# Cross-attention of layer 0: who copies keys and queries out of PSUM, and in which order three small projections are issued

## The chip, the cores and the metric

The kernel is one program on one core of one Trainium2 chip. The metric is the device time of one execution in microseconds (us). It is compared as a median of runs; the profile comes from one further execution.

## The reference, cut to what matters

A decoder of two layers on 32 batches of 100 tokens of width 256, with a context of 361 rows of width 128 for each batch. In order: self-attention, cross-attention and a mixture of experts in layer 0, then the same three in layer 1, each behind a layer norm and with a residual. The change lies in the cross-attention of layer 0 alone:

```python
Q = (x @ Wq.T).reshape(B, xN, 16, 16)
KV = (z @ Wkv.T).reshape(B, zN, 2, 16, 16)
K, V = KV[:, :, 0], KV[:, :, 1]
attn = softmax(einsum('bqhd,bkhd->bhqk', Q, K) * 0.25)
O = einsum('bhqk,bkhd->bqhd', attn, V).reshape(B, xN, 256) @ Wo.T
x = x + O
```

Sixteen heads of only 16 channels: a head fills 16 of the 128 rows of the systolic array, so the kernel packs four pairs of heads into four row groups of 32.

## The kernel before, in words

Each stage is a method; `l0_xattn` (L478 to L725) is the one that the change touches. Everything is f32.

**The two copies.** A row group of 32 channels holds two heads, "even" (j = 0) and "odd" (j = 1). Queries and keys are kept twice, as `t[:, c, 0, :]` and `t[:, c, 1, :]`. In each copy one head of the pair is kept and the other head's rows are overwritten: with zeros for queries (scale `quarter`, 0.25 or 0), with a row of ones and zeros for keys (scale `own`, bias `one`). The row of ones lets a second multiplication subtract the row maximum for nothing. `queries` (L543, 128x400 for four batches at once) and `keys` (L552, 128x361 for one batch) multiply into one PSUM bank and copy that bank out twice; before the change ScalarE makes both copies (L550, L557). `vals` (L561) is copied out by ScalarE too, in two or four pieces (L570).

**The loop** (L694) runs over M = 0 to 65; batch b = M // 2, group of eight heads c = M % 2. I call one pass a *step*. TensorE's order is exactly the order of the code (`manual_schedule` for PE). In a full step M it issues:

1. `maxima(M-1)` (L588): two transposes of the negated row maxima (L593) into one bank; VectorE adds them to the queries, giving `q2` (L595).
2. `scores(M, 0)` (L576): four matmuls of 100x361 into four banks, and four VectorE reductions (L585), one for each bank.
3. `divided(M-3)` (L636): a VectorE reciprocal (L638) and GpSimd products into `zT` (L642).
4. `turned(M-1, 0)` (L597): twelve matmuls of keys by `q2` into four banks, then four exponentials on ScalarE (L607) and two sums on GpSimd (L611, L612).
5. `values(M-2)` (L614): 24 + 8 small matmuls (L621, L628) into one bank, copied out by ScalarE (L633).
6. `scores(M, 1)` and `turned(M-1, 1)`, as above.
7. The *extras* of the step (L716). Even M: keys for group 0 of the next batch (K), the output projection of a finished tile of 128 rows (O, where one is finished: `out`, L644, whose result VectorE adds to x in L283 and whose norm statistics follow in L219 and L222), and two thirds of the values (V). Odd M: keys for group 1 (K), queries (Q, in two of every eight steps), the last third of the values (V).
8. Where something is pending in `later`, a turn of normalised rows (N: L253, copied out by `evac`, alternately by ScalarE, L172, and VectorE, L173) or the gate of the mixture of experts (G, whose VectorE part begins with L1534 and goes on with L1538 to L1547). The rows themselves are normalised by VectorE ahead of item 2 (L231, two instructions in the steps named in `norms`, L675).

**The banks.** All PSUM tiles of this stage come from one pool of eight banks (`banks("l0x", t=8)`, L481; `bank` sends every tag to "t"). A step takes 20 to 22 of them, so a bank is reused within half a step, and a matmul waits until the readers of the tile that had the bank before are done. In particular the four banks of `turned(M-1, 0)` are those of the extras of the step before and of `maxima`.

**The other queues.** ScalarE, VectorE and GpSimd each run their instructions in one fixed order, which a scheduler chose when the program was built. An instruction that waits holds up all that stand behind it on its engine.

Of the kernel before, what the change touches and what calls it, by code (L numbers as in the profile page):

```python
# [12 lines left out]
AF = mybir.ActivationFunctionType  # L13
ALU = mybir.AluOpType
# [10 lines left out]
L = 361  # L25
# [96 lines left out]
class Kernel:  # L122
# [355 lines left out]
    def l0_xattn(self):  # L478
        nc, tc, a = self.nc, self.tc, self.a
        with ExitStack() as st:  # L480
# [14 lines left out]
            for h in range(H):  # L495
# [16 lines left out]
            own, quarter, one = (  # L512
                cp.tile([P, 2], F32, tag=n, name=n) for n in ("own", "quarter", "one")
            )
# [24 lines left out]
            def load(b):  # L539
                ctx[b] = pool.tile([CD, LP], F32, tag="cT", name="cT", bufs=3)  # L540
                nc.sync.dma_start(ctx[b], a["ctxT"][:, b, :])

            def queries(b0, c):  # L543
                if c == 0:
                    q[b0 // 4] = pool.tile([P, 2, 2, 4 * T], F32, tag="qT", name="qT")
                pm = self.bank_t()[:, : 4 * T]
                self.mm(pm, [(wq[:, k, c * P : (c + 1) * P], self.xn_of(k, b0, 4)) for k in range(NK)])
                t = q[b0 // 4]
                for j in range(2):
                    nc.scalar.activation(t[:, c, j, :], pm, AF.Copy, scale=quarter[:, j : j + 1])  # L550

            def keys(b, c):  # L552
                pm = self.bank_t()[:, :L]
                self.mm(pm, [(wk[:, c * P : (c + 1) * P], ctx[b][:, :L])])
                t = ks[b % 3]
                for j in range(2):
                    nc.scalar.activation(  # L557
                        t[:, c, j, :L], pm, AF.Identity, bias=one[:, j : j + 1], scale=own[:, j : j + 1]
                    )

            def vals(b, c0, n):  # L561
                pm = self.bank_t()[:KC0, : n * D].rearrange("p (c d) -> p c d", c=n)
                for i in range(n):
                    c = c0 + i
                    self.mm(pm[:, i, :], [(ctx[b][:, c * KC0 : (c + 1) * KC0], wv)])
                pv = pm.rearrange("p c (h j d) -> p c h j d", j=2, d=16)
                v = vs[b % 3][:, c0 : c0 + n].rearrange("p c (h j) e -> p c h j e", j=2)
                for j in range(2):
                    for i in range(n):
                        nc.scalar.copy(v[:, i, :, j, 16 * j : 16 * j + 16], pv[:, i, :, j, :])  # L570
# [5 lines left out]
            def scores(M, j):  # L576
                b, c = divmod(M, 2)
                cols = slice((b % 4) * T, (b % 4 + 1) * T)
                ps = [self.bank("r")[:T, :L] for _ in range(4)]
                for r in range(4):  # L580
                    self.mm(ps[r], [(q[b // 4][rows_of(r), c, j, cols], ks[b % 3][rows_of(r), c, j, :L])])
                m = ms[M % 3]
                for r in range(4):
                    o = 32 * r + 16 * (1 - j)
                    got = nc.vector.tensor_reduce(m[:, j, o : o + 1], ps[r], AX.X, ALU.max, negate=True)  # L585
                return got

            def maxima(M):  # L588
                b, c = divmod(M, 2)
                cols = slice((b % 4) * T, (b % 4 + 1) * T)  # L590
                pt = self.bank_t()[:, : 2 * T].rearrange("p (j t) -> p j t", j=2)
                for j in range(2):
                    nc.tensor.transpose(pt[:, j, :], ms[M % 3][:, j, :], self.ident[:T, :T])  # L593
                q2[M] = pool.tile([P, 2, T], F32, tag="q2", name="q2")
                self.after = nc.vector.tensor_tensor(q2[M], pt, q[b // 4][:, c, :, cols], ALU.add)  # L595

            def turned(M, j):  # L597
                b, c = divmod(M, 2)
                ps = [self.bank("r")[:KC0, : NKC * T] for _ in range(4)]
                for i in range(NKC):  # L600
                    for r in range(4):
                        self.mm(ps[r][:, i * T : (i + 1) * T], [(
                            ks[b % 3][rows_of(r), c, j, i * KC0 : (i + 1) * KC0], q2[M][rows_of(r), j, :]
                        )])
                t = e[M, j] = pool.tile([KC0, 4, NKC, T], F32, tag="e", name="e", bufs=5)
                for r in range(4):
                    nc.scalar.activation(t[:, r], ps[r].rearrange("p (c t) -> p c t", c=NKC), AF.Exp)  # L607

                n = L - 2 * KC0
                s = es[M, j] = pool.tile([KC0, 4, T], F32, tag="es", name="es", bufs=4)  # L610
                nc.gpsimd.tensor_tensor(s, t[:, :, 0, :], t[:, :, 1, :], ALU.add)  # L611
                nc.gpsimd.tensor_tensor(s[:n], s[:n], t[:n, :, 2, :], ALU.add)  # L612
# [23 lines left out]
            def divided(M, zs, after):  # L636
                b, c = divmod(M, 2)
                got = nc.vector.reciprocal(zs[:, 1, :], zs[:, 1, :])  # L638
                if after is not None:
                    self.depend(got, [after.ins], "behind the maxima, whose banks are waited for")  # L640
                for z, cols in self.z_parts(b):
                    nc.gpsimd.tensor_tensor(z[:, c, :], zs[:, 0, cols], zs[:, 1, cols], ALU.mult)  # L642

            def out(f):  # L644
                self.out_proj(f, wo)
                self.norm_stats(f, EDGES)
# [14 lines left out]
            def extras(b):  # L661

                k0, k1, v0, v1, o, x = [None] * 6
                if b + 1 < NB:
                    k0, k1 = (lambda: keys(b + 1, 0)), (lambda: keys(b + 1, 1))
                    v0, v1 = (lambda: vals(b + 1, 0, 2)), (lambda: vals(b + 1, 2, 1))
                if b > 1 and tile_of(b - 2) is not None:
                    o = lambda: out(tile_of(b - 2))
                b0, i = b // 4 * 4, b % 4
                if i < 2 and b0 + 4 < NB:  # L670
                    x = lambda: queries(b0 + 4, i)
                return k0, v0, o, k1, v1, x
# [11 lines left out]
            with tc.manual_schedule(engines={mybir.EngineType.PE}):  # L684
                load(0)
                load(1)
                for c in range(2):
                    queries(0, c)
                for c in range(2):
                    keys(0, c)  # L690
                vals(0, 0, 2)
                vals(0, 2, 1)
                last = 2 * NB
                for M in range(last + 2):  # L694
                    b, c = divmod(M, 2)
                    if c == 0:
                        if b + 2 < NB:
                            load(b + 2)
                        ex = extras(b)
                    if 0 < M <= last:  # L700
                        maxima(M - 1)
                    if M in norms:
                        f, *at = norms[M]
                        f(*at)
                    for j in range(2):

                        got = scores(M, j) if M < last else None
                        if j == 0 and M > 2:
                            divided(M - 3, zs, got)
                        if 0 < M <= last:  # L710
                            turned(M - 1, j)
                        if j == 0 and M > 1:
                            zs = values(M - 2)
                    if M == last + 1:
                        divided(M - 2, zs, None)
                    for i in (0, 2, 1):  # L716
                        if ex[3 * c + i]:
                            ex[3 * c + i]()
                    if M not in norms or len(later) > 3:
                        for _ in range(1 + (len(later) > 3)):  # L720
                            if later:
                                later.popleft()()
                out(NF - 1)
                while later:
                    later.popleft()()  # L725
# [1496 lines left out]
```

## Time and profile before

| what | value |
|---|---|
| median of 3 runs | 2894.04 us (2893.76 to 2896.32) |
| the profiled execution | 2872.93 us, of which 2871.0 us are the profile's span |
| granted TensorE clock, mean of the span | 0.986 |
| first and last score matmul of layer 0's cross-attention | 526.0 us and 1002.3 us after the span's start |
| first transposes of the maxima, L593, to the last | 530.7 us to 1006.0 us |
| VectorE, mean of one: L585 (100x361 reduction) / L595 / L638 | 525 / 366 / 778 ns |
| ScalarE, mean of one: L557 (keys) / L550 (queries) / L607 / L570 | 679 / 621 / 426 / 298 ns |

A line of the timeline reads: start and length in us, engine, line of the kernel, operation, what it writes and reads, shape, and how many instructions were merged into the line; in brackets the idle time of the engine ahead of it and what ended it. The profiled execution is 1.9 us longer than its span (2872.93 against 2871.0). The profiled execution was 0.7% shorter than the median of the timed runs.

### The profile page before, as it was taken

Reading aid. Unit: us, or ns where it says so; the run is one execution under the profiler, and the core shown is the slowest. Engines: PE = TensorE matmul, PEld = TensorE weight load, DVE = VectorE, ACT = ScalarE, POOL = GpSimd, SP = SyncE. Lnnn points to the kernel's source line nnn. Section 1 sums busy time; section 2 is a strip of 40 time slices with the busy share of each in tenths; the row PEclk is TensorE's granted clock in tenths of the full one; section 3 lists DMA queues with packets and bytes.
Section 4 is the critical chain, followed back from the end, with each engine's and each line's share of the span. In section 5 each row is a group of like instructions: output and inputs, shape, how many; then the busy total and the mean of one; then the engine's idle time right before and its main releaser. Section 6 shows DMA issues by size and latency. Waiting matters only on the chain. (4 is left out here: it accounts for less than half of the span.)

```text
span 2871.0 us, 66274 instructions
## 1 busy us (share of the span) xinstructions
PE 2768.8 (96%) x25880; PEld 2150.2 (75%) x25880; DVE 1760.6 (61%) x5043; ACT 1391.4 (48%) x4210; POOL 920.4 (32%) x1079
## 2 busy tenths in 40 slices
PE   8999999999999999999999999999999999999992
PEld 7888888777777757888886777777777777776672
DVE  7666766677777742222225877677676676766553
ACT  5555655666667621222223225656565566567220
POOL 3222212465656544222211330021311202123473
PEclk9999999999999989999999999999999999999997
DMA  7444333000000033655652210010000000000496
GB/s 246 134 131 165 133 141 120 23 16 16 13 16 16 5 107 137 204 199 190 203 219 92 80 43 10 9 43 18 27 15 9 12 12 11 13 11 5 122 216 190
DMA packets 133877, 242.02 MB, mean 84 GB/s; under 512 B 40714, under 2 KB 105925, under 8 KB 126768
## 3 DMA queue, kind: packets, MB, share of 16 engines
q1 hardware_dynamic: 103488, 143.53, 16.0%
q0 software_dynamic: 26784, 90.83, 9.8%
q8 instruction: 209, 3.42, 0.5%
q10 hardware_dynamic: 3280, 3.28, 0.3%
q14 instruction: 116, 0.95, 0.1%
HBM read 152.12 MB, written 111.18 MB: 92 GB/s over the span
## 5 line engine op out<-in xcount | busy, mean ns | idle before, releaser
L1818 POOL DMA_INDIRECT x_d<-xr,slot x200 | 195.0, 975 | 657.4 <-ACT eT L846 595.1
L178 PE MATMUL ps_t<-xnT,wA 128*128 128x200 f32 (+1 forms) x1608 | 322.5, 348 | 2.2 <-DMA wA<-in_wq 1.6
L178 PE MATMUL ps_t<-cT,q 128*128 128x361 f32 (+1 forms) x832 | 306.1, 470 | 0.0
L846 ACT COPY eT<-ps_t 124x384 f32<-124x384 f32 x400 | 191.2, 486 | 221.1 <-PE ps_t L845 221.0
L178 PEld LDWEIGHTS ps_t<-xnT,wA 128*128 128x128 f32 x1608 | 273.0, 191 | 30.2 <-issue 14.6
L836 ACT ACTIVATE wBx<-ps_t,m 128x361 f32<-128x361 f32 x400 | 227.5, 570 | 119.5 <-DVE m L833 115.2
L585 DVE TENSOR_REDUCE m<-ps_t 100x1 f32<-100x361 f32 x512 | 239.6, 525 | 47.4 <-PE ps_t L178 47.2
L178 PE MATMUL ps_t<-xT,w 128*128 128x256 f32 (+1 forms) x1276 | 260.2, 364 | 0.7 <-ACT xT L172 0.7
L178 PEld LDWEIGHTS ps_t<-xT,w 128*128 128x128 f32 x1276 | 223.8, 190 | 36.0 <-issue 9.3
L833 DVE TENSOR_REDUCE m<-ps_t 128x1 f32<-128x361 f32 x400 | 210.9, 528 | 59.3 <-PE ps_t L178 57.1
L845 PEld LDWEIGHTS ps_t<-ident,wBx 128*124 128x124 f32 x1200 | 150.2, 139 | 117.6 <-issue 70.5
L607 ACT ACTIVATE e<-ps_t 121x300 f32<-121x300 f32 x512 | 173.9, 426 | 119.0 <-PE ps_t L178 119.0
L384 ACT ACTIVATE e<-s,m 100x100 f32<-100x100 f32 x512 | 185.6, 364 | 66.2 <-DVE m L378 66.2
L388 POOL TENSOR_TENSOR e<-e,rz 100x400 f32<-100x400 f32 x128 | 109.3, 854 | 323.8 <-PE ps_t L178 208.0
L845 PE MATMUL ps_t<-ident,wBx 128*124 128x128 f32 x1200 | 196.8, 275 | 3.6 <-DVE top L1758 2.3
L178 PE MATMUL ps_t<-wA,cT 128*124 128x512 f32 x384 | 195.6, 597 | 0.0
L1465 DVE TENSOR_TENSOR h<-ps_t,g 128x256 f32<-128x256 f32 (+1 forms) x145 | 58.3, 402 | 188.4 <-ACT g L1464 188.4
L838 DVE TENSOR_SCALAR wBx<-wBx,sums 128x361 f32<-128x361 f32 x400 | 165.4, 414 | 9.4
L178 PEld LDWEIGHTS ps_t<-q,k 32*121 32x121 f32 x3072 | 127.6, 181 | 36.1 <-issue 11.3
L1464 ACT ACTIVATE g<-ps_t 128x256 f32<-128x256 f32 (+1 forms) x145 | 52.9, 365 | 190.9 <-PE ps_t L178 190.9
L857 PEld LDWEIGHTS ps_t<-eT,v 124*64 124x64 f32 x3072 | 134.0, 137 | 13.5 <-issue 6.1
L837 DVE RECIPROCAL sums<-sums 128x1 f32<-128x1 f32 x400 | 63.8, 160 | 126.3 <-ACT wBx L836 124.8
(333 smaller groups left out, 5678.1 us busy)
## 6 DMA issues: line engine op xcount, KB each, us to landing
x_d<-fill SPq DMA_DIRECT2D x16, 1284.0 KB
we<-in_wexp SPq DMA_DIRECT2D x32, 384.0 KB
cT<-in_ctxT SPq DMA_DIRECT2D x64, 186.0 KB
xe_d<-zero SPq DMA_DIRECT2D x8, 1028.0 KB
xe<-x_d SPq DMA_DIRECT2D x24, 321.0 KB
sum<-fill SPq DMA_DIRECT2D x10, 640.0 KB
yk<-y_d SPq DMA_DIRECT2D x25, 256.0 KB
xe<-xe_d SPq DMA_DIRECT2D x24, 257.0 KB
```

Source lines behind the costliest of these rows:

```text
L178: self.nc.tensor.matmul(out, lhsT=l, rhs=r, start=(i == 0), stop=(i == n - 1))
L384: nc.scalar.activation(t[:, i, :], s[:, i, :], AF.Exp, bias=m[:, i : i + 1], accum_out=rz[:, i : i + 1])
L388: nc.gpsimd.tensor_tensor(t[:, h, :], t[:, h, :], self.last(rz[:, h], T), ALU.mult)
L585: got = nc.vector.tensor_reduce(m[:, j, o : o + 1], ps[r], AX.X, ALU.max, negate=True)
L607: nc.scalar.activation(t[:, r], ps[r].rearrange("p (c t) -> p c t", c=NKC), AF.Exp)
L833: self.after = nc.vector.tensor_reduce(m, ps, AX.X, ALU.max, negate=True)
L836: nc.scalar.activation(t, ps, AF.Exp, bias=m, accum_out=z)
L838: nc.vector.tensor_scalar(t, t, z, None, ALU.mult)
L845: nc.tensor.transpose(pt[:, c, :], es[n % 5][:, c * KC : (c + 1) * KC], self.ident)
L846: self.after = nc.scalar.copy(eT[:, :, o : o + P], pt)
L857: nc.tensor.matmul(pz[64 * j : 64 * j + 64, i, :], lhsT=v[:, c, h * 64 : (h + 1) * 64], rhs=eT[:, c, o : o + T], start=(c == 0), stop=(c = ...
L1818: got = nc.gpsimd.indirect_dma_start(out=self.x1_d[:, :], out_offset=bass.IndirectOffsetOnAxis(ap=slot[:, j, k : k + 1], axis=0), in_=xr[: ...
```

## The change

```diff
                 t = q[b0 // 4]
-                for j in range(2):
-                    nc.scalar.activation(t[:, c, j, :], pm, AF.Copy, scale=quarter[:, j : j + 1])
+                nc.scalar.activation(t[:, c, 0, :], pm, AF.Copy, scale=quarter[:, 0:1])
+                nc.vector.tensor_scalar_mul(t[:, c, 1, :], pm, quarter[:, 1:2])
...
                 t = ks[b % 3]
-                for j in range(2):
-                    nc.scalar.activation(
-                        t[:, c, j, :L], pm, AF.Identity, bias=one[:, j : j + 1], scale=own[:, j : j + 1]
-                    )
+                nc.scalar.activation(t[:, c, 0, :L], pm, AF.Identity, bias=one[:, 0:1], scale=own[:, 0:1])
+                nc.vector.tensor_scalar(t[:, c, 1, :L], pm, own[:, 1:2], one[:, 1:2], op0=ALU.mult, op1=ALU.add)
...
-                    for i in (0, 2, 1):
+                    for i in ((0, 1, 2), (2, 0, 1))[c]:
                         if ex[3 * c + i]:
                             ex[3 * c + i]()
```

The copies with j = 1 go to VectorE: 64 of keys and 16 of queries. The extras are issued in the order K, V, O in even steps (before: K, O, V) and Q, K, V in odd steps (before: K, Q, V).

The scheduler of the other engines gives VectorE a new order with it. GpSimd's and the DMA queue's orders are the same as before; ScalarE's is the same but for the copies that went, the Q and K that changed places, and a few places near the stage's end. As built, VectorE's queue from the last reduction of a step to the first of the next is (`q2` is L595, "K2" and "Q2" the new copies):

```
step                             before                            after
even, O                          L283 L219 L222 q2                 K2 L283 q2 L219
even, O and G                    L283 L219 L222 L1534 q2           K2 L283 L1534 L219 L1538 x2 L222 L1539 x2 q2
even, no O                       q2                                K2 q2
odd, Q                           q2                                Q2 q2 K2
odd, Q, rows to normalise next   q2 L231 L231                      Q2 q2 K2 L231 L231
odd, N copied by VectorE         L173 q2                           K2 L173 q2
odd, N copied by ScalarE         q2                                K2 q2
```

In the program after, K2 and Q2 carry a wait for ScalarE's semaphore: each starts only when ScalarE's copy of the same bank is done. (Of the odd steps without Q, N or G, some have K2 behind q2.)

## The prediction

> **What bounds the kernel now.** I read the page's busy shares first, then the busy times of one window, then the waits in it, and last the timeline, step by step.
>
> ```profile
> PE 2768.8 (96%) x25880; PEld 2150.2 (75%) x25880; DVE 1760.6 (61%) x5043; ACT 1391.4 (48%) x4210; POOL 920.4 (32%) x1079
> 530.46:1005.60 475.14, 464.75 (x8721) 361.75 (x8720) 359.24 (x871) 322.31 (x929) 285.64 (x361) 1.00 0.05 14
> ```
>
> TensorE (PE) bounds the whole, and this stage too: 464.75 us busy of 475.14 (the row's columns are length, PE, its weight loads, VectorE, ScalarE, GpSimd). VectorE (DVE) is busy 359 us, ScalarE (ACT) 322 us, so the change takes work from the freer engine and gives it to the fuller one. What counts is therefore only where TensorE waits for either. The longest pieces of the chain that ended last all lie behind 1531 us and say nothing of this stage, so I take the waits from 530 to 1010 us:
>
> ```profile
> PEld ps_t L178 <- DVE m L585: 9.9, 56, 0.5
> PEld ps_t L178 <- ACT v L570: 8.0, 14, 1.1
> PEld ps_t L621 <- DVE m L585: 8.0, 14, 1.4
> PE ps_t L621 <- DVE m L585: 5.7, 7, 1.2
> ...
> PEld ps_t L178 <- ACT k L557: 2.5, 6, 0.6
> ...
> PE ps_t L178 <- ACT v L570: 1.9, 10, 0.2
> ...
> PEld ps_t L178 <- ACT qT L550: 1.4, 4, 0.4
> ```
>
> The first number is us in total. On ScalarE's copies TensorE waits 8.0 + 2.5 + 1.9 + 1.4 = 13.8 us: the most that the change can give back, and 0.5% of the time. On VectorE's reductions it waits 23.6 us already. A step without stalls takes 6.5 to 7.5 us by its extras; I compared each step, cut at the first transpose of the maxima, with the shortest of its kind.
>
> **What is removed and added.** ScalarE loses 64 key copies and 16 query copies. A pair of key copies takes 1.22 us and one 0.68, so a queue step of ScalarE is 0.54 us shorter. VectorE gets 80 instructions that the trace does not show. Nearest rows: a VectorE instruction with a pointer scalar from PSUM takes 408 ns at 128x200 (L348) and 478 ns at 128x256 (L2092); extended at 1.04 ns an element that is 0.58 us for 128x361 and 0.62 for 128x400. Bounds: 0.44 (what each of four reductions of the same width in a row adds, 1.85 us in all) and 0.68 (ScalarE's copy). I take 0.58, of which the queue behind it sees 0.49, as reductions of 0.525 follow at 0.44.
>
> The new copy K2 waits for ScalarE's copy of the same bank, and that stands behind four exponentials. Here is the end of odd step 21, where VectorE also copies a turn of rows (N), and the start of step 22:
>
> ```profile
> 681.12 1.85 DVE L585 TENSOR_REDUCE m<-ps_t 100x1 f32<-100x361 f32 x4 [0.34 <-PE ps_t L178]
> ...
> 681.74 1.36 ACT L607 ACTIVATE e<-ps_t 121x300 f32<-121x300 f32 x4 [0.99 <-PE ps_t L178]
> ...
> 682.95 1.22 ACT L557 ACTIVATE k<-ps_t,one,own 128x361 f32<-128x361 f32 x2
> ...
> 683.29 0.34 PE L593 MATMUL ps_t<-ident,m 100*128 100x100 f32 x2
> 683.49 0.69 DVE L173 COPY xnT<-ps_t 128x512 f32<-128x512 f32 x1 [0.52 <-PE ps_t L253]
> ...
> 684.10 0.35 DVE L595 TENSOR_TENSOR q<-ps_t,qT 128x200 f32<-128x200 f32 x1
> ...
> 684.60 1.01 PE L178 MATMUL ps_t<-q,k 32*121 32x100 f32 x24 [0.18 <-ACT v L570]
> ```
>
> Read it as a race into q2 (L595), which TensorE's twelve `turned` matmuls (684.60) need. VectorE is free at 682.97 and idle to 683.49. K2 cannot use that gap: ScalarE's first copy ends at 682.95 + 0.68 = 683.63. So K2 runs 683.68 to 684.26, L173 goes from 683.49 to 684.17, q2 from 684.10 to 684.78.
>
> **A, N by VectorE:** q2 0.68 later, `turned` about 0.65 (it had 0.15 behind q2, 0.05 is enough). Steps 6, 14, 22, 30, 54: 3.3; step 42 (Q in front, more slack) 0.3. Together **+3.6**.
>
> **B, rows to normalise.** In step 20 q2 runs at 669.83, L231 twice from 670.23, the reductions from 670.88; the first ends at 671.40 and TensorE's `values` (L621), which take that bank, start at 671.48. After the change K2 stands between q2 and L231 and moves this by 0.49 less the slack. Steps 4, 12, 20, 28, 36, 44, 52: seven times 0.45; step 24 0.3. **+3.5**.
>
> **C, O with a gate (G).** End of step 26, start of 27:
>
> ```profile
> 722.10 1.03 PE L178 MATMUL ps_t<-wB,cT 128*121 128x256 f32 x4
> 722.30 0.42 DVE L283 TENSOR_TENSOR x_sb<-ps_t,x_sb 128x256 f32<-128x256 f32 x1 [0.51 <-PE ps_t L178]
> ...
> 723.96 0.17 DVE L1534 COPY lg<-ps_t 128x16 f32<-128x16 f32 x1 [0.55 <-PE ps_t L178]
> ...
> 724.18 0.37 DVE L595 TENSOR_TENSOR q<-ps_t,qT 128x200 f32<-128x200 f32 x1
> 724.47 0.23 DVE L1538 MAX8 top<-lg 128x8 f32<-128x8 f32 x2
> 724.66 0.09 DVE L1539 MATCH_VALUE_LOAD ti<-top,lg 128x8 f32 x1
> ...
> 724.76 0.79 PE L178 MATMUL ps_t<-q,k 32*121 32x100 f32 x24
> ```
>
> With V ahead of O, O ends where V ended, 723.13 instead of 722.26. L283 moves there, and its statistics no longer fit ahead of L1534 (it waits for G in any case). The built order then runs L219 (0.4), L1538, L222, L1539 (0.49 from 724.47 to the next reduction, and 0.1) before q2: it starts near 725.03, not 724.18. Steps 27, 43, 47: 0.8 each; 39 and 55, where VectorE was late before behind q2 and gets that part back, 0.4. **+3.2**.
>
> **D, square roots.** In steps 19, 35, 51 the norm's statistics feed a ScalarE square root ahead of the exponentials (two table loads of 1.28 us). It waits for L224, which ended at 661.93 with O first; with O last, and q2, L219, two reductions and L222 ahead of it, near 663.54. The square root ran at 663.02, so the exponentials come 0.55 later: **+1.6**.
>
> **E, O alone** (steps 7, 9, 11, 15, 17, 21, 25, 29, 33, 37, 45, 53). In step 20 L283 goes from 676.24 to 677.11, q2 ends at 677.85 instead of 677.64; `turned` started 0.21 behind q2, so 0 to 0.2 is lost. I take 0.1: **+1.2**.
>
> **What comes back.** F, the start: four query and four key copies (2.05 + 2.30 us) halve, the first scores start 0.4 us earlier, the first exponentials 0.5: -0.9. G, N copied by ScalarE (8, 16, 38, 46): TensorE loses 0.64 to K and the turn; q2 now ends 0.5 later behind K2 and takes back half: -1.2. H, steps 3, 5, 13, 41, 49 lose 0.57 to V's copies. ScalarE is earlier by 0.54, but K2 ends at 618.1 in step 12, so q2 goes from 617.50 to 618.01, the stall only changes its name: -0.5. I, steps 10, 18, 34, 50, 32, 48, 56: ScalarE's stall of 0.3 to 0.5 gone, K2 behind q2 in its place: -0.7. J, steps 40 and 60: one reduction now stands ahead of the rows: -0.9. Together **-4.2**.
>
> Sum: 3.6 + 3.5 + 3.2 + 1.6 + 1.2 - 4.2 = **+8.9 us**. Against the profiled execution that is 2872.93 to 2881.8; against the median 2894.04, which is 0.7% above that execution, 2902.9. Steps 57 to 61, with gate, root and rows at once, I leave at 0 (2 either way). GpSimd's and the DMA queue's order and work do not change; later stages start as much later as this one ends.
>
> The Trainium skill, "PSUM — Partial Sum Buffer", section "PSUM bank collisions raise a hardware error", says that two engines must not access one bank at once, reads included, so that software has to put one behind the other. It speaks against the change's idea, two copies side by side; the trace of before has no bank that both read freely. Could both read at once, K2 would fit VectorE's gap at 682.97 and A and the loss in G would be gone: the sum by that would be about +4. A second rule, "SBUF — State Buffer", section "SBUF: two separate sides", says that VectorE and GpSimd lock each other out of a shared port for some instructions; were K2 one of these, it could cost what L231 does beside GpSimd.
>
> **Rivals.** *Faster: ScalarE's relief decides.* For it: TensorE's waits on ScalarE are 13.8 us, and VectorE is idle a quarter of the stage. If they all go and only B stays, -13.8 + 3.5 = -10: 2884. Against it: the wait of K2 on ScalarE, and q2 behind K2 in VectorE's fixed queue. It decides if q2 starts no later than 0.1 us beyond its place of before in most steps.
> *Nothing:* stalls change their names as in H, and A to E are half hidden: 2891 to 2897.
> *Much slower: K2 is long.* L231 takes 412 ns in the median but up to 1286 ns in this stage beside GpSimd; L348, from PSUM, never over 427. If K2 behaves like L231 and takes 0.5 more in some 25 steps of A, B, C, H: +12, 2915.
>
> **How the numbers follow.** Forecast (sum as worked, 2897 to 2910) 0.57; much slower 0.15; nothing 0.15; faster 0.13. Bounds: K2 at 0.44 or 0.68 moves A and B by -1 to +1.5; E is 0 to 2.4; C and D could be half; G and H could give 4 more. The range, 2889 to 2914, leaves out most of the faster case and the end of the slowest. About 0.2%, 5.8 us, is what a measurement of this kernel can tell from no change. Faster by more: 0.13. Within: the nothing case and a fifth of the forecast, 0.26. Slower: 0.61.
>
> **What would show it.** In the profile after: K2 starts within 0.1 us of the end of ScalarE's key copy and takes 0.5 to 0.6; q2 ends 0.6 later in steps like 22 and 0.8 later in those like 27; TensorE's waits on L570 and L557 shrink while those on L595 and L585 grow. I am wrong if TensorE's busy time over this stage is the same and its steps are shorter, or if K2 starts ahead of ScalarE's end.

## The result and the profile after

The changed kernel takes 2900.77 us, the median of 14 runs (2897.19 to 2906.46). The kernel before, run beside it 14 times, takes 2895.76 us. The ratio is 1.0018, with a 95% interval of 1.0011 to 1.0026: 3.2 to 7.5 us slower, +5.0 in the middle. The prediction had +8.9 us, so the sign is right and the sum is too large. By the prediction's own line of 5.8 us, a change of 5.0 falls under "within" (0.26), not under "slower" (0.61); with 14 runs of each the interval nevertheless leaves zero out.

The profiled execution of after took 2904.64 us with a span of 2902.9, against 2871.0 before. This gap of 31.9 us must not be read as the change. I profiled both kernels a second time: after then spans 2875.3 us and before 2899.9. Medians of the kernel before also stand at two levels (2871.73 to 2873.08 in two sets of runs, 2895.76 to 2897.35 in the others), apparently by the chip that a set ran on (14 and 1 against 5 and 2; the chip of the first set is not on record). The two profiles of after lie 27.6 us apart with the same instructions, all of it behind this stage: 9 us between 1106 and 1134 us, 10 us between 2694 and 2712, the rest in pieces of 1 to 2 us. Each of the two large pieces holds a stretch of 10.24 us in which the first profile shows a granted clock of 0.5 and the second does not. What I compare is therefore only the stage, step by step.

First the page's busy shares of after, with the same columns as before, and then the busy times of the whole stage (528.36 to 1012.14 us, 63 steps): length, PE, PEld, DVE, ACT, POOL, granted clock, DMA share, GB/s.

```profile
PE 2777.7 (96%) x25880; PEld 2145.6 (74%) x25880; DVE 1792.0 (62%) x5123; ACT 1349.8 (46%) x4130; POOL 919.8 (32%) x1079
```

```profile
528.36:1012.14 483.78, 465.64 (x8721) 354.44 (x8720) 389.76 (x950) 282.98 (x853) 285.61 (x361) 0.99 0.05 14
```

ScalarE is 39 us less busy here (322.31 before) and VectorE 31 us more (359.24 before), as intended. The stage is 483.78 us long instead of 475.14, and TensorE's own busy time has hardly changed (465.64 and 464.75). So the loss is waiting. Of these 8.6 us, 5.1 lie in steps that are comparable between the two profiles; the rest lies in steps that hold a stretch at half clock in one of the two (see below). The waits of after from 530 to 1016 us (us in total, times, longest):

```profile
DVE k L557 <- ACT k L556: 27.3, 40, 0.8
DVE qT L550 <- ACT qT L549: 21.6, 14, 4.3
...
PEld ps_t L178 <- DVE q L593: 13.5, 34, 0.9
...
PE ps_t L178 <- DVE q L593: 9.6, 20, 0.9
...
PEld ps_t L178 <- ACT v L568: 5.6, 8, 0.9
PEld ps_t L619 <- DVE m L583: 5.6, 12, 1.4
...
PEld ps_t L178 <- DVE m L583: 4.4, 22, 0.5
...
PE ps_t L619 <- DVE m L583: 3.6, 9, 1.2
```

The lines have moved: q2 is now L593, the reductions are L583, ScalarE's key copy is L556, K2 is L557, the values' copies are L568. TensorE's wait for the values' copies fell from 8.0 us to 5.6, and its waits for reductions in the three rows above from 23.6 us to 13.6. Its wait for q2 rose from 4.9 us (4.3 and 0.6 in its two rows of before) to 23.1. This is a stall that changed its name and grew. The first row points to the cause: VectorE stands idle for 27.3 us because K2 waits for ScalarE's copy of the same bank. K2 itself took 651 ns in the mean in this stretch, Q2 634.

Here is step 22 of after, the step that the prediction worked out in detail:

```profile
687.23 0.68 ACT L556 ACTIVATE k<-ps_t,one,own 128x361 f32<-128x361 f32 x1
...
687.94 0.65 DVE L557 TENSOR_SCALAR k<-ps_t,own,one 128x361 f32<-128x361 f32 x1 [0.69 <-ACT k L556]
688.51 0.68 DVE L173 COPY xnT<-ps_t 128x512 f32<-128x512 f32 x1
689.11 0.35 DVE L593 TENSOR_TENSOR q<-ps_t,qT 128x200 f32<-128x200 f32 x1
...
689.61 0.42 PE L178 MATMUL ps_t<-q,k 32*121 32x100 f32 x5 [0.91 <-DVE q L593]
```

K2 starts 0.03 us behind the end of ScalarE's copy (687.91). The step starts at 687.46, so q2 comes 1.65 us into it; before it came at 0.92 (684.10 in a step from 683.18). TensorE waits 0.91 us for it.

**How the steps are counted.** I cut the stage at each first transpose of the maxima and subtract the lengths of before. In steps 2 to 60 the two profiles of before agree within 0.02 us, but for step 24 (0.06) and step 42 (0.17), so a tenth of a microsecond means something. Steps that contain a stretch at half clock (a granted TensorE clock of 0.5 in the trace, shown in the last section) are left out of the sums: steps 1 and 24, and 61 to 63. Two small numbers of that kind remain (step 58 in the copies-alone run below, and 58 to 60 in the second profile of after). By the prediction's terms:

```
us against before   predicted  after   copies   order    six     picks   picked   VectorE
                                       alone    alone    back    later   apart    first
A  N by VectorE       +3.6     +3.50   +3.42    -0.12    +0.03   +3.50   +0.18    -0.47
B  rows (not 24)      +3.2     +1.06   -0.14    +1.33    +0.88   +1.05   +0.09    -0.68
C  O with gate        +3.2     +3.00   +1.95    +2.99    +2.99   +3.15   -0.01    +2.99
D  square roots       +1.6     +0.06   +0.01    +0.05    +0.05   +0.06   +0.06    +0.05
E  O alone            +1.2     +0.56   +4.39    +1.87    +0.52   +0.55   +0.53    +1.89
G  N by ScalarE       -1.2     -0.90   -0.89    +0.03    -0.88   -0.89   -0.90    -1.12
H  V's copies         -0.5     -0.02   -0.05    +0.04    -0.04   -0.05   -0.16    +0.27
I  ScalarE's stall    -0.7     -0.30   +0.20    +1.59    -0.30   -0.29   -0.37    -0.72
J  rows, 40 and 60    -0.9     -0.87   -0.54    -0.07    -0.86   -0.87   -0.70    -0.06
steps 23, 31           -       +0.68   +0.68     0.00    +0.67   +1.25    0.00    -0.01
steps 2, 26            -       -0.12   -0.08    +0.87    -0.12   -0.12   -0.12    +0.14
steps 57 to 59         0       -1.58   +0.25    -0.52    -1.58   -1.61   -1.58    -0.62
sum                            +5.08   +9.18    +8.06    +1.37   +5.73   -2.98    +1.67
timed, from ratio              +5.2   +10.4     +8.4     -0.9    +5.8    -3.4     +0.9
```

The columns are the experiments that follow. The last row is the ratio to the runs of before made beside it, less one, times that median. Sum and timing agree within 2.5 us, about half the width of an interval.

### The profile page after: what moved, and what is told of

Read it like the earlier page. It is cut to its first block, busy times and chain, and to the rows that moved or that the text cites. A ratio compares the mean times of both kernels' runs of the same rounds, so it can differ in the third digit from the quotient of the medians.

```text
span 2902.9 us, 66320 instructions
## 1 busy us (share of the span) xinstructions
PE 2777.7 (96%) x25880; PEld 2145.6 (74%) x25880; DVE 1792.0 (62%) x5123; ACT 1349.8 (46%) x4130; POOL 919.8 (32%) x1079
## 5 line engine op out<-in xcount | busy, mean ns | idle before, releaser
L583 DVE TENSOR_REDUCE m<-ps_t 100x1 f32<-100x361 f32 x512 | 240.5, 524 | 28.2 <-PE ps_t L178 27.9
L178 PEld LDWEIGHTS ps_t<-q,k 32*121 32x121 f32 x3072 | 120.6, 183 | 52.4 <-issue 14.2
```

The lines of the kernel that those rows point to most:

```text
L178: self.nc.tensor.matmul(out, lhsT=l, rhs=r, start=(i == 0), stop=(i == n - 1))
```

## The experiments

**Theory Q**, held at the start: the time goes where q2 stands behind something new in VectorE's queue, above all K2 with its wait. **Rival O**: the new order alone makes the loss. **Rival C**: the copies alone make it. A third rival was that nothing in the steps changed and the clock made the difference.

### Copies alone

```diff
-                    for i in ((0, 1, 2), (2, 0, 1))[c]:
+                    for i in (0, 2, 1):
```

> The changed kernel with the old order of the projections (keys, output, values), so only the copies by VectorE are left. Theory Q (the time goes where q2, the sum that TensorE's next exponents need, stands behind something new in VectorE's queue): the gate's part (+3.0 us) and the statistics' part (+0.6) go, the six steps with a key copy in front of the turned norm keep their +3.5 and the rows' steps their +1.0, the start, the V steps and the last key steps keep their -3.3; the key copy now stands ahead of the output's sum in 23 steps, at 0 to 0.15 each: +1 to +4 us against the kernel before in all, 1 to 4 us faster than the changed kernel. Rival O (the new order alone makes the loss): 0 or below against before. Rival C (the copies alone make the loss): +5, as the changed kernel.

Measured: 1.0036 (1.0022 to 1.005), about +10.4 us: worse than the whole change, which none of the theories had. (The interval overlaps that of the whole change; the steps, +9.2 against +5.1, are clear.) A is there as expected. The miss is E: +4.39 in twelve steps that end up behind an output, 0.25 to 0.38 each where I had at most 0.15. Two timelines of the end of step 6 show it, first copies alone, then the changed kernel:

```profile
575.56 0.65 DVE L557 TENSOR_SCALAR k<-ps_t,own,one 128x361 f32<-128x361 f32 x1 [0.69 <-ACT k L556]
576.13 0.41 DVE L283 TENSOR_TENSOR x_sb<-ps_t,x_sb 128x256 f32<-128x256 f32 x1
576.57 0.43 DVE L219 BATCH_NORM_STATS2 st<-x_sb 128x6 f32<-128x256 f32 x1
576.92 0.35 DVE L593 TENSOR_TENSOR q<-ps_t,qT 128x200 f32<-128x200 f32 x1
```

```profile
576.22 0.65 DVE L557 TENSOR_SCALAR k<-ps_t,own,one 128x361 f32<-128x361 f32 x1 [0.69 <-ACT k L556]
576.91 0.43 DVE L283 TENSOR_TENSOR x_sb<-ps_t,x_sb 128x256 f32<-128x256 f32 x1
577.25 0.36 DVE L593 TENSOR_TENSOR q<-ps_t,qT 128x200 f32<-128x200 f32 x1
```

Step 7 starts at 575.82 in the first and at 576.49 in the second. With the old order the output's product is done early, but its sum L283 stands behind K2, and q2 behind both and L219: 1.10 us into the step. With the new order the product ends later anyway, K2 fits ahead of it, L219 goes behind q2, and q2 comes at 0.76. Before, it came at 0.59. So the new order hides K2, and L219 no longer stands ahead of q2.

### Order alone

The kernel before, with the edit above the other way round. 

> The kernel before with the new order of the odd sets alone; both copies stay on ScalarE. Theory Q: the gate's steps (27, 39, 43, 47, 55) lose 3.0 us as in the changed kernel, the statistics' 13 steps 0.6, nothing in steps 6, 14, 22, 30, 42, 54, and the start as before: +3 to +4 us against the kernel before. Rival O: +5. Rival C: 0.

Measured: 1.0029 (1.002 to 1.0038), about +8.4 us, by the steps (+8.1) again worse than both together. C is +2.99 and A is gone, as expected; E and I are larger. The waits of this kernel (530 to 1016 us):

```profile
PEld ps_t L178 <- ACT v L570: 15.0, 28, 1.1
...
PEld ps_t L178 <- ACT k L557: 5.2, 18, 0.6
...
PEld ps_t L178 <- DVE q L595: 2.7, 8, 0.8
```

TensorE waits 15.0 us for the values' copies, 8.0 before and 5.6 in the changed kernel. The values come right behind the keys now, so their copies stand behind two key copies on ScalarE; with one key copy they do not hurt. Each half of the change thus pays for a cost of the other half: alone they cost 10.4 and 8.4 us, together 5. Rivals O and C fall as they were put: each had one of the halves at 0 or below when alone. Theory Q had the right place in A and C, but its sums for the two halves (at most +4) fall too.

### Six key copies given back

```diff
+                if 2 * (b - 1) + c in (5, 13, 21, 29, 41, 53):
+                    nc.scalar.activation(t[:, c, 1, :L], pm, AF.Identity, bias=one[:, 1:2], scale=own[:, 1:2])
+                else:
                     nc.vector.tensor_scalar(t[:, c, 1, :L], pm, own[:, 1:2], one[:, 1:2], op0=ALU.mult, op1=ALU.add)
```

> The changed kernel with the second key copy given back to ScalarE in six turns only (M = 5, 13, 21, 29, 41, 53), those whose copy stands ahead of the turned norm's copy and q2 on VectorE; nothing else moves on any queue of VectorE. Theory Q: the six steps lose their +3.5 us again, less up to 1 us that ScalarE's longer queue may cost: 2.5 to 3.5 us faster than the changed kernel, +1.5 to +2.5 against before. Rival (the loss lies in ScalarE and VectorE sharing their banks everywhere, or in the clock): within 0.5 us of the changed kernel, since 58 of 64 key copies stay.

Measured: 0.9997 (0.9988 to 1.0006), about -0.9 us. The six steps are back at the length of before (A +0.03), and no other term moves by more than 0.2. Step 22 of this kernel starts at 684.14:

```profile
684.44 0.69 DVE L173 COPY xnT<-ps_t 128x512 f32<-128x512 f32 x1 [0.51 <-PE ps_t L253]
685.05 0.35 DVE L596 TENSOR_TENSOR q<-ps_t,qT 128x200 f32<-128x200 f32 x1
...
685.55 1.01 PE L178 MATMUL ps_t<-q,k 32*121 32x100 f32 x24 [0.18 <-ACT v L571]
```

q2 comes 0.91 us into the step, as before the change. Six of 64 key copies make 3.5 us by the steps, most of the loss. By the timing this kernel is 6 us faster than the changed one, more than was expected; the steps do not show where the other 2.4 us would be, and the intervals of the two timings are wide enough for it.

### The gate's picks behind q2

The gate's `max` and `max_index` and what follows (L1536 on) are written into a function of their own, which the loop calls behind the next `maxima`, with a dependency on q2:

```diff
+                        while held:
+                            self.picks0(*held.popleft(), self.after)
...
+            got = nc.vector.max(top[:, f + j, :], lg[:, f + j, :])
+            if after is not None:
+                self.depend(got, [after.ins], "behind the queries of the next step")
```

> The changed kernel with the gate's picks (Max, MaxIndex and what follows) written behind the next turn's q2, so that they no longer stand ahead of it in steps 27, 39, 43, 47 and 55. Theory Q: these five steps lose their +3.0 us: 2 to 3 us faster than the changed kernel, +2 to +3 against before. Rival (the five steps are longer because TensorE does the values' product ahead of the output's, or because the output's sum comes later): within 0.5 us of the changed kernel.

Measured: 1.002 (1.0011 to 1.0029), about +5.8 us: nothing gained, and here theory Q fails. The rival named beforehand, that the output's product or its sum comes later, fits: C stays at +3.15 (+3.00 in the changed kernel). Step 27 starts at 725.28:

```profile
725.99 0.35 DVE L593 TENSOR_TENSOR q<-ps_t,qT 128x200 f32<-128x200 f32 x1
...
726.49 0.89 PE L178 MATMUL ps_t<-q,k 32*121 32x100 f32 x24
...
730.75 0.97 PEld L178 LDWEIGHTS ps_t<-xnT,wB 128*128 128x128 f32 x4 [0.50 <-DVE m L583]
```

q2 is indeed earlier, 0.71 us into the step against 1.20 in the changed kernel. The gain is lost at the end of the step, where TensorE waits 0.50 us for a reduction. My second guess was that VectorE is full only because it has the copies as well, so I tried the same edit on top of the order alone.

> The new order alone, both copies on ScalarE, with the gate's picks behind the next turn's q2. Theory Q in its second form (two covers in the gate's steps: picks ahead of q2, and VectorE full once it has the copies too): with no copies on VectorE the deferred picks find room, steps 27, 39, 43, 47 and 55 lose most of their +3.0 us, 2 to 3 us faster than the new order alone. Rival (the steps are long because the output's product comes later on TensorE): within 0.5 us of the new order alone.

Measured: 1.0026 (1.0015 to 1.0036), about +7.5 us, and C is +3.16: that guess fell too, and again the rival fits, by which the output's product comes later. The busy times of step 47, before and then after, point to the reason (the third number behind the length is VectorE's):

```profile
874.96:880.82 5.86, 5.86 (x137) 4.81 (x137) 5.49 (x23) 2.93 (x11) 1.85 (x3) 1.00 0.01 3
```

```profile
880.38:886.80 6.42, 6.01 (x137) 4.49 (x137) 5.79 (x25) 2.59 (x8) 2.15 (x4) 1.00 0.01 3
```

In this step VectorE was busy for 5.49 of 5.86 us already. TensorE and VectorE are both nearly full there. After the change VectorE is idle for 0.63 of 6.42 us, so being full is not the whole account. In the old order the output's statistics L219 and L222 (0.43 and 0.18 us) ran in the step before, while VectorE waited for the logits; in the new order the output's sum comes 0.86 us later and they fall into the full step.

### The statistics ahead of the logits

On top of the changed kernel with the picks behind q2: the logits' copy depends on the output's `bn_stats`, q2 on the logits' copy, and the first reductions on q2, in those five steps only.

```diff
+        self.depend(got, [self.bn.ins], "behind the last output's statistics")
...
+                if M in gated:
+                    self.depend(self.after, [self.logits.ins], "behind the step's logits")
```

> The changed kernel with VectorE's queue in the five gate's steps ordered by hand as it was before: the output's sum, its two statistics, the logits' copy, q2, then the reductions and picks. Theory S (formed from the two runs with the picks deferred): in steps 27, 39, 43, 47 and 55 VectorE is busy without a gap from the logits on, and the new order puts the statistics (0.42 and 0.16 us) from an idle stretch ahead of the logits behind them. With the output's sum done 0.37 us ahead of the logits, 0.37 of these 0.58 us go back into the idle stretch: each of the five steps loses 0.3 to 0.4 of what it had gained, 1.5 to 2 us in all against the changed kernel. Rival (the picks ahead of q2, as predicted): the same 3 us as with the picks deferred stay, since q2 is no earlier than there; within 0.5 us of the changed kernel.

Measured: 1.0007 (0.9998 to 1.0016), about +2.0 us. By the steps the answer is mixed. Steps 27, 43 and 47 are at +0.35, +0.34 and +0.35 instead of +0.57, +0.56 and +0.57: the direction is right, the size of 0.22 each is short of 0.3 to 0.4. Step 39 does not gain (+1.12 for +0.98), and step 55 gets worse (+1.05 for +0.33). The sum over the steps (+6.1) is no better than the changed kernel's +5.1, while the timing is 3 us better; I cannot bring the two together. For 27, 43 and 47 the moved statistics are shown to be part of the cause, 0.22 us of 0.57. What makes the other 0.35 us there, and the loss of steps 39 and 55, stays open.

### VectorE's copy first

VectorE's copy is written ahead of ScalarE's, for queries and keys, so that ScalarE waits for VectorE.

```diff
+                nc.vector.tensor_scalar(t[:, c, 1, :L], pm, own[:, 1:2], one[:, 1:2], op0=ALU.mult, op1=ALU.add)
                 nc.scalar.activation(t[:, c, 0, :L], pm, AF.Identity, bias=one[:, 0:1], scale=own[:, 0:1])
-                nc.vector.tensor_scalar(t[:, c, 1, :L], pm, own[:, 1:2], one[:, 1:2], op0=ALU.mult, op1=ALU.add)
```

> The changed kernel with VectorE's copy written ahead of ScalarE's for keys and queries, so that ScalarE waits for VectorE and not the other way round. Theory Q: VectorE's key copy starts about 0.7 us earlier and the six steps with the turned norm lose their +3.5; the key copy stands behind the norm's rows (up to -1.0), but ahead of q2 in twelve odd steps with queries (0 to +0.2 each), and ScalarE's value copies come 0.65 later (0 to +1.5): 1 to 4 us faster than the changed kernel. Rival (it is the copy's own length on VectorE that counts, not its wait): within 1 us of the changed kernel.

Measured: 1.0003 (0.9994 to 1.0011), about +0.9 us, 4 us better than the changed kernel. A goes from +3.50 to -0.47. E rises to +1.89 and J's gain is lost: ScalarE is now the one that waits (530 to 1016 us), and its values' copies come late again.

```profile
ACT k L557 <- DVE k L556: 17.9, 31, 3.8
...
PEld ps_t L178 <- ACT v L568: 17.3, 41, 1.1
```

### The parts that pay, alone

From the step table I took the change back where it costs: K2 returns to ScalarE in 18 turns, and the five turns with a gate's output keep the old order.

```diff
+            gated = (26, 38, 42, 46, 54)
+            both = (3, 5, 11, 13, 19, 21, 22, 29, 30, 35, 41, 51, 53) + gated
...
-                    for i in ((0, 1, 2), (2, 0, 1))[c]:
+                    for i in (0, 2, 1) if M in gated else ((0, 1, 2), (2, 0, 1))[c]:
```

> The changed kernel with each part of the change taken back in the turns where the trace shows it to cost: the second key copy back to ScalarE in 18 turns (ahead of the turned norm's copy, of the norm's rows, of the gate's logits), and the old order in the five turns with a gate's output (26, 38, 42, 46, 54). Theory Q: what is left of the steps' differences is the gains (steps 8, 28, 44 -0.28 each, 40 -0.55, 57 to 60 -1.9, small ones -0.7) and eight statistics steps at +0.05: -3 to -4.5 us against the kernel before, 8 to 9 us faster than the changed kernel. Rival (the gains hang on ScalarE being relieved everywhere, so they go with the copies taken back): within 1.5 us of the kernel before.

Measured: 0.9988 (0.9978 to 0.9997), about -3.4 us: this kernel beats the changed one clearly, and the one before by an interval that just leaves 1 out. A, B and C are at +0.18, +0.09 and -0.01, and the gains in G, J and the last steps stay. They do not need ScalarE's relief everywhere.

### The wait or the length

In 13 of those turns VectorE makes the copy after all, and makes it first.

```diff
+                if M in first:
+                    nc.vector.tensor_scalar(t[:, c, 1, :L], pm, own[:, 1:2], one[:, 1:2], op0=ALU.mult, op1=ALU.add)
                 nc.scalar.activation(t[:, c, 0, :L], pm, AF.Identity, bias=one[:, 0:1], scale=own[:, 0:1])
```

> The kernel with the parts taken back (e5_pick), but in the 13 turns ahead of the turned norm, the rows and the logits without an output VectorE makes the second key copy after all, and makes it first: ScalarE's copy waits for it, not the other way round. In the six turns M = 5, 13, 21, 29, 41, 53 VectorE's queue is then that of the changed kernel word for word (key copy, turned norm's copy, q2), only without the wait. If the wait made the cost (as the prediction has it), steps 6, 14, 22, 30, 42 and 54 are no longer than before, 0 to -0.15 us each, against +0.26 to +0.82 in the changed kernel; in all 1 to 2 us faster than e5_pick, -4 to -6 us against the kernel before. If the copy's own 0.65 us in the queue made it, they are +0.4 or more each, in all 2 us slower than e5_pick.

Measured: 0.9989 (0.998 to 0.9998), about -3.2 us, the same as the kernel it was made from and not 1 to 2 us better. For A the answer is clear: steps 6, 14, 22, 30 and 54 are at 0.00, -0.12, -0.12, -0.12 and -0.12, and 42 at +0.14. Step 22 starts at 686.51 here:

```profile
686.23 0.64 DVE L561 TENSOR_SCALAR k<-ps_t,own,one 128x361 f32<-128x361 f32 x1
686.82 0.69 DVE L173 COPY xnT<-ps_t 128x512 f32<-128x512 f32 x1
...
687.43 0.35 DVE L602 TENSOR_TENSOR q<-ps_t,qT 128x200 f32<-128x200 f32 x1
```

It is the same queue (K2, L173, q2) and K2 is as long, but it runs in the gap that VectorE had before, and q2 is back at 0.92 us. So the wait of 0.69 us makes term A, because with it K2 misses that gap, and not the copy's own 0.65 us. The rest of the expectation missed: in the turns ahead of the norm's rows K2 now stands ahead of q2, and B is +1.89.

### Both kernels once more

> The changed kernel once more, for a second profile: if the length of its steps is a property of the program, each of the 63 steps agrees with the first profile within 0.05 us except where the granted clock was halved; the span then differs from 2902.9 us only by the stretches at half clock. If the first profile's 6.8 us at half clock in step 1 was chance, it is gone here.

> The kernel before once more, for a second profile beside the one above: each of its 63 steps agrees with the first profile's within 0.05 us but for those at half clock, and what its span differs by lies outside the stage, as between the two profiles of the changed kernel.

The steps repeat: after within 0.09 us but for step 24 and steps 58 and 59, which are touched by half clock, before as told above. The 6.8 us at half clock in step 1 came again in the second profile of after. They come in the last kernel above too, and in none of the other kernels, five of which have the same instructions up to there. Whether the change brings them or only their moment stays open.

## Why the prediction was partly right

- **The mechanism of A was right in place and in size.** +3.50 measured for +3.6. K2 waited for ScalarE's copy as predicted, and the two runs on the six turns show the wait as the cause, from both sides.
- **K2's price** was low: 0.58 us estimated, 0.651 measured, inside the bounds of 0.44 to 0.68. The two rows that it was drawn from are 70 ns apart over 56 columns, 1.25 ns each; with that slope in place of 1.04 it would have been 0.61. It was not long like L231, so the much slower rival fell.
- **B was the term most out in size:** +1.06 for +3.2 (without step 24, which is at -0.11 where both profiles have half clock). Steps 4, 12, 20, 36 and 52 lose 0.17 to 0.42, which is near the 0.45; but steps 28 and 44 gain 0.28 each. Step 28, before and then after:

```profile
731.80 1.03 POOL L612 TENSOR_TENSOR es<-es,e 119x400 f32<-119x400 f32 x1
731.85 1.45 DVE L231 TENSOR_SCALAR wAn<-x_sb,mv,rstd 128x256 f32<-128x256 f32 x2
```

```profile
735.52 1.03 POOL L610 TENSOR_TENSOR es<-es,e 119x400 f32<-119x400 f32 x1
735.79 0.65 DVE L557 TENSOR_SCALAR k<-ps_t,own,one 128x361 f32<-128x361 f32 x1
736.36 0.73 DVE L231 TENSOR_SCALAR wAn<-x_sb,mv,rstd 128x256 f32<-128x256 f32 x2
```

L231 took 1.45 us beside GpSimd's sum. K2 takes 0.65 us beside the same sum and holds L231 back until that is nearly over, and then L231 takes 0.73. I had priced the delay and not what the rows are delayed past. That is the step that failed in B: "moves this by 0.49 less the slack". The sign given beforehand, that TensorE's waits for the reductions grow, also came out the other way (23.6 us before, 13.6 after). The Trainium skill, "SBUF — State Buffer", section "SBUF: two separate sides", has a lock between the two engines for some instructions; the rows fit it for L231, and K2, which reads PSUM, was not slowed (643 to 655 ns in all 64).
- **C was right in size (+3.00 for +3.2) by luck and wrong in cause.** Steps 27, 43 and 47 lost 0.57 each for 0.8, step 39 lost 0.98 and step 55 0.33 for 0.4 each. The step that failed is to take q2's delay ("it starts near 725.03, not 724.18") as the loss. q2 was late as told (1.20 us into step 27, before 0.52), but q2 in time gives nothing back. The new order alone makes the whole term (+2.99). The statistics that it moves into these steps are shown for 0.22 us in three of them; the rest, some 2.3 of 3.0 us, is open.
- **D was wrong:** +0.06 for +1.6. The step that failed is L224's end, "with O last, and q2, L219, two reductions and L222 ahead of it, near 663.54". The square root of step 19, before and then after:

```profile
660.87 1.03 POOL L612 TENSOR_TENSOR es<-es,e 119x400 f32<-119x400 f32 x1
...
661.39 0.54 DVE L224 TENSOR_SCALAR rstd<-mv 128x6 f32<-128x6 f32 x1
...
663.02 0.21 ACT L225 ACTIVATE rstd<-rstd 128x6 f32<-128x6 f32 x1
```

```profile
664.68 1.03 POOL L610 TENSOR_TENSOR es<-es,e 119x400 f32<-119x400 f32 x1
...
666.64 0.16 DVE L224 TENSOR_SCALAR rstd<-mv 128x6 f32<-128x6 f32 x1
666.83 0.21 ACT L225 ACTIVATE rstd<-rstd 128x6 f32<-128x6 f32 x1 [0.86 <-DVE rstd L224]
```

The step starts at 660.52 before and at 664.32 after, so the root comes at 2.50 and at 2.51. L224 starts 2.32 us into the step, near the 2.48 that I feared, but takes 0.16 us instead of 0.54. This is B's miss again: before, L224 ran beside GpSimd's sum and ended 0.03 us behind it (661.93 and 661.90), and after, the sum is over at 665.71, before L224 starts. Steps 35 and 51 show the same lengths (0.55 and 0.54, then 0.16). The root had been waiting for its table load and now waits 0.86 us for L224, and the slack is just used up: that it is used up so exactly is luck.
- **E** was 0.04 to 0.05 a step, not 0.1 (+0.56 for +1.2). **G and J** came as told (-0.90 for -1.2, -0.87 for -0.9); **I** was half (-0.30 for -0.7). **H** gave nothing (-0.02 for -0.5), the stall only changed its name.
- **F**, the start, was told as -0.9. In the kernels with the same first steps and no half clock there, step 1 ends between 0.7 us earlier and 0.1 us later than before. In the changed kernel itself it ends 1.1 to 1.9 us later, with the half clock.
- **Not priced:** steps 23 and 31, where K2 stands ahead of the logits on a full VectorE (+0.68; before, they take 5.86 us each, below the 6.5 that the prediction gave as the least for a step without stalls), and the end of the stage (-1.58), which I left at 0 with 2 either way.

The prediction's sum was about 4 us too large. B and D alone were 4 us too large (2.1 for the seven steps of B, 0.4 for step 24, 1.5 for D); the other misses nearly cancel, which is luck. The rival "faster" fell at its own condition: q2 starts 0.73 us later in step 22, 0.17 later in step 7, and more than 0.1 later in 42 of the 64 steps. Its gain exists, though: without A, B and C the change is worth -3.4 us.

## What to carry to other kernels

A copy handed to a second engine that has to wait for the first engine's copy delays everything behind it in that engine's queue. In five steps here 0.69 us of waiting cost 0.6 to 0.8 us each, and the same copy without the wait cost nothing. A delay is not yet a loss, though: in the five steps of H q2 came 0.6 us later as well, and they kept their length. A busy share over a stage (VectorE 76%) hides single steps in which the engine has 0.37 us left of 5.86; look at the steps into which work moves. Two edits may each cover the other's cost, so neither can be judged alone: 10.4 and 8.4 us apart were 5 us together, and taking both back turn by turn gave a kernel faster than either.

## What the runs showed of the hardware

In the first profile of after the granted clock falls to a half for stretches of 3.41, 6.83 and 10.24 us, multiples of 3.41, but for the last one, at the program's end. Here are the stretch in step 1 of after and the 3.41 us ahead of it:

```profile
528.86:532.27 3.41, 2.32 (x36) 1.57 (x37) 3.00 (x8) 2.60 (x7) 0.00 (x0) 1.00 0.00 0
...
532.27:539.10 6.83, 6.83 (x37) 4.94 (x36) 2.65 (x6) 2.46 (x8) 4.11 (x4) 0.50 0.01 2
```

TensorE is busy for 2.32 us of the first row and for all of the second, with a granted clock of 0.50 in the second. Step 1 is 2.6 us longer with it (11.29 us against 8.65 in the kernels with the same first steps), and a stretch of 3.41 us in step 24 costs about 1.7. So a wait may cost a second time, behind itself; which waits do is not shown. The Trainium skill, "TensorE: Matmul & The Clock Gate", section "What's actually happening", has half rate after an idle one of free-running windows of 3413 ns. The length agrees. A window of after with TensorE busy for 68% was enough here, and one with 2.17 of 3.41 us in step 24 of the same profile (702.94 to 706.35, a whole number of 3.41 us behind the first) was not, so what counts as idle stays open.

Two profiles of one kernel can differ by 27.6 us in span while the steps of a stage agree within some hundredths.
